# A perceiver layer on one core: another table of pieces for the last units of cross-attention, and weights converted by ScalarE

## The chip, the cores and the metric

The kernel runs on one core of a Trainium2 chip. The metric is the device time of that core in microseconds. Times shown are medians of several runs; durations of single instructions come from one profiled execution.

## The reference, cut to what matters

Four batches of 256 query tokens (width 256) pass through three blocks, each with a residual sum. The arrays are float32.

```
x = x + cross_attention(layernorm(x), ctx, ctx)       # 16 heads of 16, 4096 context rows
x = x + feature_attention(layernorm(x))               # 16 heads, causal
x = x + feed_forward(layernorm(x))                    # hidden 768, int32 weights times 1/127
```

In feature attention queries and keys of each head are divided by their norm over the head's 16 numbers, `x / max(norm(x), 1e-12)`, then projected, shifted, clipped and exponentiated. The feed-forward weights `w_gate`, `w_up`, `w_down` come as int32 and are made float32 and scaled before their matmuls.

## The kernel before, in words

The work is written out in order by hand: TensorE (PE), VectorE (DVE), ScalarE (ACT) and SyncE (SP) run their instructions in the order of the source.

**Cross-attention** goes over 16 units (batch b, group q of four heads), each of 16 steps of 256 context rows, so there are 256 steps n = 0 to 255 and one more for what is left. In a step TensorE makes the scores `pt` (L741) and, 18 steps ahead of them, the products `pm` (L704) from which VectorE takes maxima (L711). ScalarE turns the scores into `e` by an exponential (L746). TensorE multiplies the `e` of the step before by the values into `pav` (L761), and VectorE sums it into `av` (L771, at a unit's first step L769). Steps from 238 on have no `pm`, because the last unit's maxima are done by then. The keys and values of later units are made between these, up to step 231. From step 232 one entry of the table `others` runs in each step; the table belongs to feature attention of batches 0 to 2, which is begun here, and its layer norms were done before. A unit's result is divided (`pt_x` L787, L791, L793) two steps into the next unit.

The pieces of the table, for batch b with tiles 2b and 2b+1 of 128 tokens:

- `turn`: four transposes of the normed rows (L198), copied by VectorE (L199).
- `qk(i)`: the matmuls `pqk` (L207), the bias by VectorE (L211), and the squares on GpSimd (L213).
- `sq(i)`: sums of squares by head, VectorE (L216).
- `v`: the matmuls of the values (L225), biases by VectorE (L230).
- `normed_pair(b)`: `normed` for both tiles, 13 small VectorE instructions (L241, L123 to L129, L245) that turn the sums of squares into inverse norms by shifts and three iterations.
- `qk_normed(t)`: queries and keys of a tile times their inverse norms, VectorE (L249).
- `qk_turned(t)`: four transposes (L254), copied by VectorE (L255).
- `features(n)`: sixteen matmul instructions into four banks `pf` (L271), clipped by VectorE (L277), exponentials on ScalarE (L278), a factor on GpSimd (L279).

In PSUM, `bank` gives out eight banks of one pool in turn, so a tile waits until the one eight allocations before it has been read.

**Attention and feed-forward** follow in 16 steps `attend(n)` and one more. TensorE makes `pa` (L407, L412), VectorE masks it into `at` (L417), TensorE makes `po` (L426), ScalarE copies it to `avT` (L431), TensorE turns that (`pt_o`, L438) and VectorE divides (L440 to L442). Between the steps lie the lists `fills[n]`: in `fills[1]` to `fills[3]` the weights are converted by `weight(0)` to `weight(2)` (L390), in `fills[2]` and `fills[3]` the last projection of cross-attention is finished (`px` L811 with its copy L812, `py` L819, sum L822) and the layer norm of batch 3 is made (L139 to L147, which contain the same small iterations L123 to L129), in `fills[4]` the turn and queries and keys of batch 3 follow. All three weights arrive through the one buffer `w_i`; a load (L51) is issued on SP's queue, and the next one only when the conversion before it has read the buffer.

Of the kernel before, what the change touches and what calls it, by code (L numbers as in the profile page):

```python
# [14 lines left out]
AF = mybir.ActivationFunctionType  # L15
ALU = mybir.AluOpType
# [23 lines left out]
def perceiver_layer(  # L40
# [5 lines left out]
    nc = tc.nc  # L46
# [69 lines left out]
    def inverse_root(v):  # L116


        y = lnp.tile(list(v.shape), F32, tag=f"ir_y{v.shape[1]}", name="ir_y")
        t = lnp.tile(list(v.shape), F32, tag=f"ir_t{v.shape[1]}", name="ir_t")  # L120

        def first():
            nc.vector.tensor_scalar(y.bitcast(I32), v.bitcast(I32), 1, None, ALU.arith_shift_right)  # L123
            nc.vector.tensor_scalar(y.bitcast(I32), y.bitcast(I32), -1, 0x5F3759DF, ALU.mult, ALU.add)

        def better():
            nc.vector.tensor_tensor(t, y, y, ALU.mult)
            nc.vector.scalar_tensor_tensor(t, t, -0.5, v, ALU.mult, ALU.mult)
            nc.vector.scalar_tensor_tensor(y, t, 1.5, y, ALU.add, ALU.mult)  # L129

        return y, [first, better, better, better]
# [106 lines left out]
    def normed(tiles):  # L238

        some = nrm[:, tiles[0] : tiles[-1] + 1, :].rearrange("p t h -> p (t h)")  # L240
        nc.vector.tensor_scalar(some, some, 1e-24, None, ALU.max)  # L241
        y, pieces = inverse_root(some)
        for piece in pieces:
            piece()
        nc.vector.tensor_copy(some, y)  # L245
# [35 lines left out]
    def start_causal():  # L281


        zs = [causal_in(b) for b in range(B - 1)]
        n = 2 * (B - 1)
        mv = lnp.tile([P, n, 2], F32, tag="ln_mv6", name="ln_mv6", bufs=1)
        v = lnp.tile([P, n], F32, tag="ln_v6", name="ln_v6", bufs=1)
        rs, roots = inverse_root(v)
        s2 = lnp.tile([P, R], F32, tag="s2", name="s2", bufs=1)
        rs2, roots2 = inverse_root(s2)  # L290

        def constants():


            nc.gpsimd.memset(va, 1.0)
            nc.vector.tensor_scalar(top, rest[6], 20.0, None, ALU.add)
            nc.vector.tensor_scalar(low, rest[6], -20.0, None, ALU.add)
            nc.vector.tensor_scalar(shift, rest[6], -1.0, None, ALU.mult)
            nc.vector.tensor_scalar(fac, rest[7], 0.0, 1.0 / M, ALU.max, ALU.mult)
            nc.vector.tensor_scalar(s2, rest[10][:, : R * M : M], 0.0, 2.0, ALU.max, ALU.mult)  # L300

        def scaled():

            nc.vector.tensor_tensor(s2, s2, rs2, ALU.mult)
            om = rest[5].rearrange("p k (r m) -> p (k r) m", m=M)
            for i in range(4):
                to = om[:, R * i : R * i + R, :]
                nc.vector.tensor_tensor(to, to, s2.unsqueeze(2).to_broadcast([P, R, M]), ALU.mult)

        def stats(t):  # L310
            st = lnp.tile([P, 6], F32, tag="ln_st", name="ln_st")
            nc.vector.bn_stats(st, xr[:, t, :])
            nc.vector.bn_aggr(mv[:, t, :], st)
            nc.vector.tensor_scalar(v[:, t : t + 1], mv[:, t, 1:2], LN_EPS, None, ALU.add)

        def normal(t):
            nc.vector.tensor_scalar(
                zs[t // 2][5][:, t % 2, :], xr[:, t, :], mv[:, t, 0:1], rs[:, t : t + 1], ALU.subtract, ALU.mult
            )
            nc.gpsimd.tensor_tensor(xr[:, t, :], xr[:, t, :], rest[9], ALU.add)  # L320

        norms = (
            [lambda t=t: stats(t) for t in range(n)] + roots + [lambda t=t: normal(t) for t in range(n)]
            + [constants] + roots2 + [scaled]
        )

        (_, turn0, qk0, sq0, v0, _), (_, turn1, qk1, sq1, v1, _), (_, turn2, qk2, sq2, v2, _) = zs

        def normed_pair(b):
            return lambda: normed((2 * b, 2 * b + 1))  # L330

        def call(f, *args):
            return lambda: f(*args)

        others = [
            [turn0],
            [call(qk0, 0)],
            [call(qk0, 1), call(sq0, 0)],
            [v0, call(sq0, 1)],
            [turn1, normed_pair(0)],  # L340
            [call(qk1, 0), call(qk_normed, 0)],
            [call(qk1, 1), call(sq1, 0), call(qk_normed, 1)],
            [v1, call(sq1, 1)],
            [call(qk_turned, 0), normed_pair(1)],
            [call(qk_turned, 1), turn2, call(qk_normed, 2)],
            [call(features, 0), call(qk_normed, 3)],
            [call(features, 2)],
            [call(qk2, 0)],
            [call(qk2, 1), call(sq2, 0)],
            [v2, call(sq2, 1)],  # L350
            [call(qk_turned, 2), normed_pair(2)],
            [call(qk_turned, 3), call(qk_normed, 4)],
            [call(qk_turned, 4), call(qk_normed, 5)],
            [call(qk_turned, 5)],
            [call(features, 4)],
        ]
        return norms, [call(lambda pieces: [piece() for piece in pieces], pieces) for pieces in others]

    finish = cross_attention(
        tc, xr, load_x, load_rest, ctxT, wq_sb, bq_sb, wkP, bk_sb, wvP, eps, ident, layernorm, transposed,  # L360
        qT, kts, lnp, bank, rest, start_causal)
    wout_sb = rest[8]

# [19 lines left out]
    coming = []  # L383

    def weight_load(i):
        src = (w_gate, w_up, w_down)[i]
        coming.append(load(src, list(ws[i].shape), "w_i", mybir.dt.int32, nc.sync, late))

    def weight(i):
        nc.gpsimd.tensor_scalar(ws[i], coming[i], (1.0, 0.5, 1.0)[i] / 127.0, None, ALU.mult)  # L390
        if i + 1 < len(ws):
            weight_load(i + 1)

# [115 lines left out]
    with tc.manual_schedule(engines={ET.PE, ET.Activation, ET.DVE, ET.SP}):  # L509
# [4 lines left out]
        fills = {n: [] for n in range(NB + 1)}  # L514
        norm3, turn3, qk3, sq3, v3, _ = causal_in(3)
        fills[1] += [lambda: weight(0)]
        fills[2] += [turn15, lambda: weight(1)]
        fills[3] += [project15, norm3, lambda: weight(2)]
        fills[4] += [turn3, lambda: qk3(0)]
        fills[5] += [lambda: qk3(1), lambda: sq3(0), v3, lambda: sq3(1), lambda: normed((6, 7))]  # L520
# [4 lines left out]
        def call(b, part, *args):  # L525
            return lambda: ff[b][part](*args)
# [531 lines left out]
```

## Time and profile before

| what | value |
|---|---|
| median of 3 runs | 1243.35 us (1241.18 to 1244.96) |
| profiled execution, its own time | 1243.55 us |
| its span, first to last instruction | 1241.8 us |
| mean granted TensorE clock | 0.989 |
| TensorE matmuls, busy | 1205.1 us (97%) |
| VectorE, busy | 932.3 us (75%) |
| ScalarE, busy | 669.6 us (54%) |
| GpSimd, busy | 71.4 us (6%) |
| first piece of `others`, step 232 | about 987 us |
| last unit, steps 240 to 255 | 1029.87 us to about 1084 us |
| conversions of the weights on GpSimd | 3 of 4.09 us, from 1096.0, 1104.3 and 1112.6 us |

Times inside the profile count from the first instruction of the span. A row of a timeline has start, length, engine, line, operation, output and inputs, and in brackets how long the engine was idle before it and what ended that. The granted clock is the share of full speed that TensorE had.

### The profile page before, as it was taken

How to read it: one execution, taken by the hardware profiler on the slowest of the kernel's cores; microseconds unless marked ns; L12 is line 12 of the kernel's file. 1: busy time of each engine (PE TensorE's matmuls, PEld its weight loads, DVE VectorE, ACT ScalarE, POOL GpSimd, SP SyncE). 2: the span in 40 equal slices, each digit the busy share in tenths (PEclk: the TensorE clock that was granted, in tenths of full speed). 3: DMA queues.
4: the chain of work that ended last, by engine and by line, in shares of the span. 5: the costliest groups of instructions: out<-in, count | busy, mean ns of one | idle time of the engine just before them, and what ended most of it. 6: DMA issues, size and time to landing. Idle time of an engine off the chain costs nothing.

```text
span 1241.8 us, 42115 instructions
## 1 busy us (share of the span) xinstructions
PE 1205.1 (97%) x17712; PEld 809.0 (65%) x17712; DVE 932.3 (75%) x1823; ACT 669.6 (54%) x1391; POOL 71.4 (6%) x118
## 2 busy tenths in 40 slices
PE   6999999999999999999999999999999999969998
PEld 3566667666766676667666766677667745536777
DVE  4787777777777777777777777777788866597763
ACT  2446666666665656566566666666566536731311
POOL 4010000000000000000000000000001012151100
PEclk8999999999999999999999999999999989989999
DMA  6351342233223322332233223322332000020000
GB/s 227 105 179 59 103 117 71 60 103 105 85 60 102 114 77 58 102 107 80 61 94 101 87 68 90 102 89 72 88 103 88 5 1 4 2 79 1 9 10 18
DMA packets 57756, 95.78 MB, mean 77 GB/s; under 512 B 29024, under 2 KB 31712, under 8 KB 57568
## 3 DMA queue, kind: packets, MB, share of 16 engines
q1 hardware_dynamic: 56384, 92.17, 24.5%
q8 instruction: 140, 2.29, 0.8%
q10 hardware_dynamic: 672, 0.92, 0.2%
q14 instruction: 48, 0.39, 0.1%
q0 software_dynamic: 512, 0.00, 0.0%
HBM read 74.17 MB, written 1.05 MB: 61 GB/s over the span
## 4 chain that ended last, share of the span: by engine, by line
PE 91%; DVE 5%; ACT 1%; issue 1%; DMA 1%; SPq 0%; ACTq 0%; POOL 0%; DVEq 0%
PE pt L741 21%; PE pm L704 18%; PE pav L761 18%; PE pv L668 10%; PE pk L638 10%; PE pd L500 2%; PE pg L488 1%; PE pu L488 1%; PE pqk L207 1%; PE pq L844 1%; PE po L426 1%; DVE at L417 1%; PE pa L407 1%; PE py L462 1%; DVE kt L277 1%
## 5 line engine op out<-in xcount | busy, mean ns | idle before, releaser
L711 DVE TENSOR_REDUCE mx<-pm 128x1 f32<-128x512 f32 x1024 | 636.0, 684 | 146.6 <-PE pm L704 146.6
L746 ACT ACTIVATE e<-pt 128x512 f32<-128x512 f32 x1024 | 528.9, 603 | 390.1 <-PE pm L704 363.8
L704 PE MATMUL pm<-kt,qT 32*128 32x512 f32 x2048 | 500.3, 618 | 4.7 <-ACT ku L646 2.4
L741 PE MATMUL pt<-qa,kt 32*128 32x256 f32 x4096 | 501.1, 388 | 1.2 <-DVE qa L727 1.0
L741 PEld LDWEIGHTS pt<-qa,kt 32*128 32x128 f32 x4096 | 316.4, 184 | 118.4 <-ACT v L675 43.2
L761 PE MATMUL pav<-e,v 128*32 128x256 f32 x4096 | 270.3, 380 | 0.0
L704 PEld LDWEIGHTS pm<-kt,qT 32*128 32x128 f32 x2048 | 172.1, 184 | 22.5 <-issue 4.9
L761 PEld LDWEIGHTS pav<-e,v 128*32 128x32 f32 x4096 | 128.9, 110 | 74.6 <-ACT e L746 5.1
L771 DVE TENSOR_TENSOR av<-pav,av 128x256 f32<-128x256 f32 x240 | 101.7, 424 | 64.8 <-PE pav L761 64.5
L638 PE MATMUL pk<-ctx,wk_sb 128*32 128x256 f32 x2048 | 138.6, 392 | 0.0
L668 PE MATMUL pv<-wv_sb,ctx 128*32 128x128 f32 x4096 | 137.5, 276 | 0.0
L668 PEld LDWEIGHTS pv<-wv_sb,ctx 128*32 128x32 f32 x4096 | 104.3, 109 | 43.9 <-DVE mx L711 43.1
L638 PEld LDWEIGHTS pk<-ctx,wk_sb 128*32 128x32 f32 x2048 | 55.3, 111 | 69.3 <-DVE mx L711 41.9
L646 ACT ACTIVATE ku<-pk,bk_sb 128x256 f32<-128x256 f32 x128 | 63.1, 495 | 15.2 <-PE pk L638 6.5
L798 POOL TENSOR_TENSOR on<-on,bv_sb 128x64 f32<-128x64 f32 x32 | 9.2, 308 | 816.5 <-DVE on L793 816.5
L675 ACT COPY v<-pv 128x256 f32<-128x256 f32 x128 | 51.8, 405 | 7.5 <-PE pv L668 7.5
L278 ACT ACTIVATE kt<-kt,shift 128x512 f32<-128x512 f32 x32 | 22.8, 724 | 30.1 <-DVE kt L277 30.1
L417 DVE TENSOR_TENSOR at<-pa,mask 128x384 f32<-128x384 f32 x64 | 31.1, 549 | 7.0 <-PE pa L412 7.0
L277 DVE TENSOR_SCALAR kt<-pf,low,top 128x512 f32<-128x512 f32 x32 | 23.7, 802 | 3.2 <-PE pf L271 3.2
L488 PE MATMUL pg<-zT,wg 128*128 128x256 f32 x96 | 23.0, 382 | 0.7 <-ACT zT L480 0.7
L492 ACT ACTIVATE th<-pg 128x512 f32<-128x512 f32 x12 | 7.1, 594 | 29.9 <-PE pg L488 29.9
L488 PE MATMUL pu<-zT,wu 128*128 128x256 f32 x96 | 22.7, 379 | 0.0
(126 smaller groups left out, 584.7 us busy)
## 6 DMA issues: line engine op xcount, KB each, us to landing
ctx<-in_ctxT_dram SPq DMA_DIRECT2D x128, 512.0 KB
kt<-ku SPq DMA_DIRECT2D x500, 32.0 KB
xo<-on SPq DMA_DIRECT2D x128, 8.0 KB
xr<-in_x_dram SPq DMA_DIRECT2D x4, 256.0 KB
out_dram<-o SPq DMA_DIRECT2D x8, 128.0 KB
wqkv_sb<-in_wqkv_dram SPq DMA_DIRECT2D x1, 768.0 KB
w_i<-in_w_gate_dram SPq DMA_DIRECT2D x1, 768.0 KB
w_i<-in_w_up_dram SPq DMA_DIRECT2D x1, 768.0 KB
```

The costliest lines, as they stand in the source:

```text
L417: nc.vector.tensor_tensor(at, pa, mask, ALU.mult)
L488: nc.tensor.matmul(ps[:, i, :], lhsT=w[:, k, ns], rhs=zT[:, k, :], start=k == 0, stop=k == KC - 1)
L638: nc.tensor.matmul(pk[32 * j : 32 * j + 32, :], lhsT=wk_sb[:, k, m * P + 32 * j : m * P + 32 * j + 32], rhs=x[:, k, cs], start=k == 0, sto ...
L646: nc.scalar.activation(ku[:, cs], made.pop(), AF.Identity, bias=bk_sb[:, m : m + 1])
L668: nc.tensor.matmul(pv[32 * j : 32 * j + 32, i, :], lhsT=x[:, k, t0 + 32 * j : t0 + 32 * j + 32], rhs=wv_sb[:, k, m * P : (m + 1) * P], sta ...
L675: nc.scalar.copy(to.rearrange("p t (h d) -> p t h d", d=HD + 1)[:, :, :, :HD], made.pop().rearrange("p t (h d) -> p t h d", d=HD),)
L704: nc.tensor.matmul(pm, lhsT=qT[rows, q, t0 : t0 + P], rhs=kt[rows, c * CH : (c + 1) * CH], start=True, stop=True,)
L711: nc.vector.tensor_reduce(mx[:, i, j, c : c + 1], pm, AX.X, ALU.max)
L741: nc.tensor.matmul(pt[:, i, :], lhsT=kt[rows, ks], rhs=qa[rows, :], start=True, stop=True)
L746: nc.scalar.activation(e, pt, AF.Exp, scale=0.25)
L761: nc.tensor.matmul(pav[32 * h : 32 * h + 32, :], lhsT=v[:, t % KT, c0 : c0 + 32], rhs=es[n, h][:, i, :], start=i == 0, stop=i == 1,)
L771: nc.vector.tensor_tensor(avs[u], pav, avs[u], ALU.add)
```

## The change

The table of pieces is another: `normed_pair` and `qk_normed` of the first three batches all stand in the last unit (entries 8 and later, steps 240 and later), with their turns and features moved to fit; entry 16 is empty. And `weight(i)` is computed by ScalarE as a scaled copy instead of by GpSimd.

```
@@ the table others, entries 4 and later
-            [turn1, normed_pair(0)],
-            [call(qk1, 0), call(qk_normed, 0)],
-            [call(qk1, 1), call(sq1, 0), call(qk_normed, 1)],
+            [turn1],
+            [call(qk1, 0)],
+            [call(qk1, 1), call(sq1, 0)],
             [v1, call(sq1, 1)],
-            [call(qk_turned, 0), normed_pair(1)],
-            [call(qk_turned, 1), turn2, call(qk_normed, 2)],
-            [call(features, 0), call(qk_normed, 3)],
-            [call(features, 2)],
-            [call(qk2, 0)],
+            [turn2, normed_pair(0)],
+            [call(qk2, 0), call(qk_normed, 0), call(qk_normed, 1)],
+            [call(qk_turned, 0), call(qk_turned, 1), normed_pair(1)],
+            [call(features, 0)],
+            [call(features, 2), call(qk_normed, 2), call(qk_normed, 3)],
             [call(qk2, 1), call(sq2, 0)],
             [v2, call(sq2, 1)],
-            [call(qk_turned, 2), normed_pair(2)],
-            [call(qk_turned, 3), call(qk_normed, 4)],
-            [call(qk_turned, 4), call(qk_normed, 5)],
-            [call(qk_turned, 5)],
+            [call(qk_turned, 2), call(qk_turned, 3), normed_pair(2)],
+            [],
+            [call(qk_normed, 4), call(qk_normed, 5)],
             [call(features, 4)],
+            [call(qk_turned, 4), call(qk_turned, 5)],
         ]
@@ weight(i)
-        nc.gpsimd.tensor_scalar(ws[i], coming[i], (1.0, 0.5, 1.0)[i] / 127.0, None, ALU.mult)
+        nc.scalar.activation(ws[i], coming[i], AF.Copy, scale=(1.0, 0.5, 1.0)[i] / 127.0)
         if i + 1 < len(ws):
             weight_load(i + 1)
```

## The prediction

> **What bounds the kernel now.** I read the busy shares first: TensorE's row has 97%, VectorE's 75%, ScalarE's 54%, and in the chain that ended last TensorE holds 91%. So only what stops or slows TensorE can move the end. Then I read the clock row of the 40 slices. It falls below 9 in two places, and both are where the diff works. Windows cut at the start of steps 237, 238, 239 and 240 of cross-attention, and one over attention's start, show them (columns: stretch, length, busy time of PE, PEld, DVE, ACT, POOL, granted clock, DMA):
>
> ```profile
> 1010.33:1021.51 11.18, 8.92 (x48) 3.48 (x44) 7.38 (x22) 2.17 (x4) 0.28 (x1) 0.69 0.01 1
> 1021.51:1025.87 4.36, 4.36 (x42) 2.02 (x38) 1.96 (x6) 2.07 (x4) 1.50 (x2) 1.00 0.00 0
> 1025.87:1029.87 4.00, 4.00 (x41) 2.58 (x40) 2.72 (x7) 2.06 (x4) 0.62 (x1) 1.00 0.00 0
> ...
> 1084.42:1124.83 40.41, 27.84 (x228) 17.85 (x228) 31.79 (x69) 10.64 (x18) 21.35 (x22) 0.83 0.19 61
> ```
>
> Step 237 takes 11.18 us. Step 233 holds the same TensorE work (scores, maxima, one `pqk`) and took 4.96 us in another such window. The timeline says why (start, length, instruction, idle time before it and its releaser):
>
> ```profile
> 1010.99 0.18 DVE L241 TENSOR_SCALAR nrm<-nrm 128x64 f32<-128x64 f32 x1
> ...
> 1014.00 0.20 DVE L245 COPY nrm<-ir_y 128x64 f32<-128x64 f32 x1
> 1014.11 0.42 DVE L771 TENSOR_TENSOR av<-pav,av 128x256 f32<-128x256 f32 x1
> ...
> 1014.58 1.21 PE L704 MATMUL pm<-kt,qT 32*128 32x512 f32 x1 [2.26 <-DVE av L771]
> ...
> 1016.58 3.78 PE L207 MATMUL pqk<-wqkv_sb,zT 128*128 128x512 f32 x4
> ```
>
> The 13 instructions of `normed` (L241 to L245) hold VectorE for 3.1 us; the sum behind them (L771) empties a PSUM bank that `pm` needs; TensorE stands 2.26 us, and then `pqk` runs 3.78 us where it takes 1.98 elsewhere. In attention:
>
> ```profile
> 1091.33 0.35 ACT L431 COPY avT<-po 128x256 f32<-128x256 f32 x1
> ...
> 1096.00 4.09 POOL L390 TENSOR_SCALAR wg<-w_i 128x1536 f32<-128x1536 int32 x1 [4.01 <-DMA w_i<-in_w_gate_dram]
> ...
> 1100.48 0.35 ACT L431 COPY avT<-po 128x256 f32<-128x256 f32 x1
> ...
> 1104.30 4.09 POOL L390 TENSOR_SCALAR wu<-w_i 128x1536 f32<-128x1536 int32 x1 [4.21 <-DMA w_i<-in_w_up_dram]
> ...
> 1104.43 3.98 DVE L124 TENSOR_SCALAR ir_y<-ir_y 128x2 int32<-128x2 int32 x1
> ...
> 1112.49 2.07 PE L271 MATMUL pf<-qT,om_sb 32*128 32x256 f32 x10 [7.01 <-DVE at L417]
> ```
>
> Two columns of VectorE work last 3.98 us, exactly until GpSimd's conversion of `wu` ends; TensorE stands 7.01 us behind it.
>
> **What the Trainium skill says.** (1) "SBUF — State Buffer", section "SBUF: two separate sides": VectorE (in its two-port modes) and GpSimd share a port pair under an exclusive lock that the first holds for its whole instruction; ScalarE has its own. The 3.98 us agree. (2) "TensorE: Matmul & The Clock Gate", "What's actually happening": the clock halves after an idle window of about 3.4 us and returns after a busy one, and windows run free. Narrow windows agree: the clock is 0.50 from 1013.97 to 1020.8, two windows of 3.41. But the window that dropped it was still about half busy; stops of 1.5 and 1.6 us (before 1091.73 and 1100.88) dropped nothing. (3) "ScalarE: Activation LUTs", "What ACT_TABLE_LOAD costs": 186 ns + 0.833 ns per element for immediate scale, so 1.47 us for 1536. The trace's 1024-element copy (L899) took 1.034 us, which fits.
>
> **The change, part one: the table.** No instruction is added or removed; the moved ones issue no DMA, and SP and POOL keep their order except for the squares of `qk2`'s first half, which come earlier.
> Step 237 loses the 3.1 us of VectorE: 11.18 becomes 4.96, −6.2 (2.3 + 1.5 of standing, the rest half clock). Steps 238 and 239 keep their TensorE work: 0.
> Steps 240 to 244, 19.36 us before, I replayed by hand, in times of before. Pieces: scores 1.07, `pav` 1.00, `pqk` 1.92, one `tr_qk` or turn 0.6, `pf` 1.0, `pt_x` 0.4; eight banks in turn, so a tile waits for the one eight allocations earlier. 240: turn 2.67, VectorE in `normed` to 1035.4. 241: `pqk`, 4.0. 242: two `tr_qk` and `pt_x`, 3.6, to 1040.1. VectorE then does two copies and the second `normed` until 1042.6 and the sum and division until 1043.4, and the third and fourth `pf` of step 243 need those banks: TensorE stands about 1.5 + 0.4 us, and 243 takes 5.2. 244 (features, two L249): 4.0. Sum 19.4: the stop is paid for by stops of the old order that are gone. 245 and 246 are unchanged.
> From 247 to the last `pav`: the third `normed` stops step 249's scores for 1.3 us, but features(4) comes a step earlier. From there ScalarE is the bound: six groups of exponentials at 2.06 and four L278 (2.65) make 15.0 us, started at 1066.5 instead of 1067.3, and with fewer gaps: −1.0.
> Sum of part one −7.2; half a clock drop behind 243's stop (one window of 3.4 us costs up to 1.7, covered in part by VectorE) +0.5: **−6.7**.
>
> **Part two: the weights.** Removed: 3 × 4.09 us on POOL and the lock: 3.8 on L124 and four later operations at 0.42 instead of 0.16, so 4.8 us of VectorE. Added: 3 × 1.47 on ScalarE, in order, each waiting for a DMA. `wg` lands at 1096.0, so the second `avT` (L431) behind it goes from 1093.45 to 1097.4, and `pt_o`, `pf` and VectorE's L277 behind that come 2.5 to 3 us late (TensorE stands 3.0; its clock probably drops). SP issues `w_up` at 1097.5; it lands 4.2 us later, hidden by L278, which ends at 1102.7. `wu` runs to 1104.2, so the third `avT` is at 1104.2, not 1100.48; `project15` and its sum (L822) at 1106.0 instead of 1102.5. The norm takes 4.75 us from there instead of 9.4: L417 starts at 1110.75 against 1111.89: −1.1. `wd` (issue 1104.3, landing 1108.5) frees the fourth `avT` at 1110.3, before VectorE wants it. With a halved clock from 1098 on the chain is 0.8 later. Both ends: −1.1 to +2.3 (clock low throughout). I take **−0.3**. Behind `w_down` SP has only outputs 50 us later; features(8)'s L279 on POOL come earlier, and nobody waits for them.
>
> Sum −7.0. The profiled execution took 1243.55 (span 1241.8 + 1.75 around it), 0.2 over the median: 1236.5 less that 0.2 is 1236.4.
>
> **The rivals.**
> A, as worked out: 1236.4, its own range 1233 to 1240. 66%.
> B, ScalarE's waits cost more than the lock: stops at `wg` and `wu` keep the clock low until 1118; `pf`, `px`, `po`, `pa` and `py` behind `wg` take 10 us instead of 5, L417 starts 2.3 late, so −6.7 + 2.3: 1239.0. For it: any 3 us stop fills most of a window. Against: VectorE bounds this stretch. 13%.
> C, the table does not do what it says: 237 stays long because its four maxima and bias additions (L711, L211), not `normed`, hold the bank. Then only −1.0 and −0.3 remain: 1242.1. Against: steps 233 to 235 have both and run at 4.9. 6%.
> D, slower: the stall only moves. If the second and third `normed` each stop TensorE for 2.3 us, in 243 and 249, instead of 1.5 and 1.3, the clock falls both times and each costs the 6.2 us seen in 237: −6.2 + 12.4 − 0.3 gives 1249.3. It decides from about 1.7 us idle within one window. Against: no maxima wait in these steps, and 240 to 242 held one `normed` before with 0.24 us of stop. 8%.
> E, the clock stays up and the gaps close: −6.2, −2.0 after step 247, −1.1, and the 1.9 us of standing in 243 gone: 1232.2. 7%.
>
> **How the numbers follow.** What a measurement here tells from no change is 0.3%, 3.7 us. Faster by that: most of A, half of B, E: 0.77. Within: the rest of A and B, and C: 0.15. Slower: D, 0.08. Range 1232 to 1242: from E to C, leaving out D.
>
> **What would show it.** Right: step 237 near 5 us at clock 1.00; 240 to 244 near 19.4, with one `pf` wait of 1.5 to 2 us on L771; L124 at 0.17 to 0.2 us everywhere; L390 on ACT at 1.47; a TensorE wait of about 3 us on `avT` near 1091; 1084.42 to 1124.83 (40.4 us) within a microsecond. Wrong: a clock of 0.5 in steps 243 to 250, or attention's start over 42 us. The whole forecast falls if 237 stays above 7 us.

## The result and the profile after

The changed kernel takes 1236.09 us (median of 5 runs, 1233.88 to 1238.65) against 1243.35 of the kernel before on the same chip (5 runs, 1241.18 to 1244.96): a ratio of 0.9942, 95% interval 0.9924 to 0.9960, so 7.2 us less. The profiled execution took 1238.65, the longest of the five, with a span of 1236.9 and a mean granted clock of 0.993.

First the windows of the changed kernel, cut at the same places as before: step 237; steps 240 to 244; steps 245 and 246; from step 247 to attention's start; and from there to the first `po` of the fifth step (columns: stretch, length, busy time of PE, PEld, DVE, ACT, POOL, granted clock, DMA share, GB/s). The last seven lines cut attention along a grid of 3.41 us, of which more at the end.

```profile
1012.85:1017.93 5.08, 5.08 (x48) 2.83 (x44) 4.24 (x8) 2.06 (x4) 0.06 (x1) 1.00 0.01 3
1026.29:1046.06 19.77, 18.71 (x214) 10.68 (x210) 16.75 (x46) 12.82 (x24) 3.83 (x7) 1.00 0.04 5
1046.06:1054.35 8.29, 8.29 (x80) 4.68 (x77) 5.71 (x12) 6.71 (x13) 4.07 (x5) 1.00 0.02 2
1054.35:1081.54 27.19, 25.98 (x341) 14.94 (x337) 14.22 (x35) 20.93 (x40) 2.33 (x5) 1.00 0.01 2
1081.54:1119.95 38.41, 25.45 (x229) 16.30 (x229) 27.33 (x69) 14.65 (x21) 9.39 (x19) 0.96 0.19 64
...
1090.09:1093.50 3.41, 1.95 (x23) 1.41 (x17) 2.14 (x5) 0.64 (x1) 0.00 (x0) 1.00 0.50 204
1093.50:1096.91 3.41, 2.26 (x28) 1.41 (x32) 1.39 (x4) 1.10 (x2) 0.00 (x0) 1.00 0.39 144
1096.91:1100.33 3.42, 1.92 (x28) 1.43 (x20) 3.42 (x7) 3.24 (x5) 1.70 (x4) 1.00 0.21 86
1100.33:1103.74 3.41, 2.09 (x24) 1.34 (x24) 2.42 (x8) 1.27 (x2) 0.21 (x1) 1.00 0.44 139
1103.74:1107.15 3.41, 1.51 (x17) 1.23 (x16) 2.89 (x17) 1.74 (x2) 0.00 (x0) 1.00 0.23 94
1107.15:1110.57 3.42, 2.67 (x22) 1.61 (x22) 3.35 (x10) 0.00 (x0) 1.51 (x2) 1.00 0.02 5
1110.57:1113.98 3.41, 0.31 (x1) 0.30 (x2) 3.04 (x5) 2.88 (x4) 1.49 (x4) 1.00 0.00 0
```

The reader sees step 237 at 5.08 us with TensorE busy all through it, where it was 11.18 at a clock of 0.69, and attention's start at 38.41 us and clock 0.96, where it was 40.41 and 0.83. The three stretches between them are not shorter. Cut in the same way in every kernel (from the first `pt` of a step, `pt_x` of the last unit and `po` of attention's fifth step), the table of stretches is, in us:

| kernel | 237 | 240 to 246 | 247 to attention | attention's start |
|---|---|---|---|---|
| before | 11.18 | 27.34 | 27.20 | 40.42 |
| changed | 5.08 | 28.06 | 27.19 | 38.41 |
| changed, second profile | 5.09 | 28.06 | 27.18 | 38.38 |
| table alone | 5.09 | 28.06 | 27.18 | 40.09 |
| weights alone | 11.50 | 27.35 | 27.20 | 40.41 |
| before, GpSimd in quarters | 9.85 | 27.35 | 27.20 | 36.87 |
| changed, weights one list later | 5.09 | 28.06 | 27.18 | 37.20 |
| new table, GpSimd in quarters | 5.09 | 28.06 | 27.18 | 36.20 |

All else is level, but for the first unit. In the changed kernel's profile the clock is 0.50 from 83.16 to 89.98, far from any edit, and step 237 starts at 1012.85 where it started at 1010.34. So the two spans, 4.9 apart, are 7.4 of gain less 2.5 lost at the start. The second profile of the same kernel has no such loss: step 237 starts at 1008.74, and its span is 1232.8, so nearly all of the 4.1 us between these two profiles lies at the start. The kernel before lost clock at its start too, from 24.10 to 30.93: its clock row has an 8 in the first slice, a third low place beside the two that the prediction counted.

The timeline of the changed kernel (start, length, engine, instruction, idle time before it and its releaser), first around steps 237, 242 and 243, then after step 247, then in attention:

```profile
1015.02 1.98 PE L207 MATMUL pqk<-wqkv_sb,zT 128*128 128x512 f32 x4
...
1032.73 2.13 DVE L249 TENSOR_TENSOR kt<-kt,nrm 128x512 f32<-128x512 f32 x2
1032.96 1.35 POOL L213 TENSOR_TENSOR sq<-kt 128x512 f32<-128x512 f32 x1 [10.05 <-DVE kt L211]
...
1038.80 0.69 PE L271 MATMUL pf<-qT,om_sb 32*128 32x256 f32 x2 [0.31 <-ACT e L746]
1039.43 0.42 DVE L771 TENSOR_TENSOR av<-pav,av 128x256 f32<-128x256 f32 x1
1039.90 1.12 PE L271 MATMUL pf<-qT,om_sb 32*128 32x256 f32 x10 [0.41 <-DVE av L771]
...
1064.21 2.06 ACT L746 ACTIVATE e<-pt 128x512 f32<-128x512 f32 x4 [0.41 <-PE pt L741]
...
1071.06 2.06 ACT L746 ACTIVATE e<-pt 128x512 f32<-128x512 f32 x4 [0.37 <-PE pt L741]
1073.53 4.14 ACT L746 ACTIVATE e<-pt 128x512 f32<-128x512 f32 x8 [0.41 <-PE pt L741]
...
1092.86 1.48 ACT L390 ACTIVATE wg<-w_i 128x1536 f32<-128x1536 int32 x1 [4.06 <-DMA w_i<-in_w_gate_dram]
1094.24 0.35 ACT L431 COPY avT<-po 128x256 f32<-128x256 f32 x1
...
1094.65 0.44 PE L438 MATMUL pt_o<-ident,avT 128*128 128x128 f32 x2 [2.61 <-ACT avT L431]
...
1099.88 1.47 ACT L390 ACTIVATE wu<-w_i 128x1536 f32<-128x1536 int32 x1
...
1101.65 0.44 PE L438 MATMUL pt_o<-ident,avT 128*128 128x128 f32 x2 [2.82 <-ACT avT L431]
1102.99 0.42 DVE L822 TENSOR_TENSOR xr<-py,xr 128x256 f32<-128x256 f32 x1
1104.94 0.17 DVE L124 TENSOR_SCALAR ir_y<-ir_y 128x2 int32<-128x2 int32 x1
...
1107.56 1.95 DVE L417 TENSOR_TENSOR at<-pa,mask 128x384 f32<-128x384 f32 x4
...
1113.67 3.51 PE L207 MATMUL pqk<-wqkv_sb,zT 128*128 128x512 f32 x4 [3.79 <-DVE zT L199]
```

`pqk` of step 237 takes 1.98 us, not 3.78, and nothing waits before it. In attention one wait of 7.0 us has become two of 2.6 and 2.8. PE's list of waits (engine, operation, releaser: us in total, times, longest), of which one line stands below, shows the exchange: `pf` behind `at`, 7.0 before, is gone, as is `pm` behind `av`, 2.3 before, and `pt_o` behind ScalarE's `avT` has grown from 3.7 us to 9.5.

```profile
PE pt_o L438 <- ACT avT L431: 9.5, 5, 2.8
```

### The profile page after: what moved, and what is told of

Same layout as the page of the kernel before. It is cut to its first block, busy times and chain, and to the rows that moved or that the text cites. A ratio compares the mean times of both kernels' runs of the same rounds, so it can differ in the third digit from the quotient of the medians.

```text
span 1236.9 us, 42097 instructions
## 1 busy us (share of the span) xinstructions
PE 1200.7 (97%) x17712; PEld 808.3 (65%) x17712; DVE 928.3 (75%) x1823; ACT 673.2 (54%) x1394; POOL 60.2 (5%) x115
## 4 chain that ended last, share of the span: by engine, by line
PE 92%; DVE 4%; DMA 1%; ACT 1%; issue 1%; SPq 0%; ACTq 0%; POOL 0%; DVEq 0%
PE pt L741 22%; PE pm L704 18%; PE pav L761 18%; PE pv L668 11%; PE pk L638 10%; PE pd L500 2%; PE pg L488 1%; PE pu L488 1%; PE pq L844 1%; PE pqk L207 1%; PE po L426 1%; PE pa L407 1%; PE py L819 1%; PE py L462 1%; PE pf L271 0%
## 5 line engine op out<-in xcount | busy, mean ns | idle before, releaser
L711 DVE TENSOR_REDUCE mx<-pm 128x1 f32<-128x512 f32 x1024 | 636.1, 684 | 149.2 <-PE pm L704 149.1
L417 DVE TENSOR_TENSOR at<-pa,mask 128x384 f32<-128x384 f32 x64 | 31.1, 549 | 7.0 <-PE pa L412 7.0
```

Source lines behind the costliest of these rows:

```text
L417: nc.vector.tensor_tensor(at, pa, mask, ALU.mult)
L711: nc.vector.tensor_reduce(mx[:, i, j, c : c + 1], pm, AX.X, ALU.max)
```

## The experiments

The medians of the kernel before, run beside these kernels, were 1242.2 to 1243.8 us. Each ratio is against the runs of the kernel before on the same chip. It is not the ratio of the medians: the two differ by up to 0.0022 in what follows.

**The table alone** (the weights stay on GpSimd):

```
-        nc.scalar.activation(ws[i], coming[i], AF.Copy, scale=(1.0, 0.5, 1.0)[i] / 127.0)
+        nc.gpsimd.tensor_scalar(ws[i], coming[i], (1.0, 0.5, 1.0)[i] / 127.0, None, ALU.mult)
```

> The new table alone, the weights still on GpSimd. Theory: the two parts add, and the table gives what the traces show for steps 237 to 255: 237 takes 5.1 us instead of 11.2, steps 240 to 246 cost 0.7 us more, the rest is level, so about 5.4 us faster than before (1238), with L124 still at 4 us in attention. The prediction's own sum for this part was 6.7 us. Rival: most of the gain is ScalarE's conversion, and the table gives 3 us or less.

Measured: 1236.56 us, ratio 0.9965 (0.9952 to 0.9979). Step 237 is 5.09, attention's start 40.09. The timeline of this kernel shows the same lock with another victim:

```profile
1096.10 4.02 DVE L123 TENSOR_SCALAR ir_y<-ln_v 128x2 int32<-128x2 int32 x1
1100.15 0.43 DVE L124 TENSOR_SCALAR ir_y<-ir_y 128x2 int32<-128x2 int32 x1
...
1104.40 2.07 PE L271 MATMUL pf<-qT,om_sb 32*128 32x256 f32 x10 [7.04 <-DVE at L417]
```

Here `wu` runs on GpSimd from 1096.00 to 1100.09, and L123, one instruction earlier than L124, lasts 4.02 us; L124 itself is 0.43. TensorE's wait of 7.04 us is unchanged. So the lock falls on whichever small instruction comes next, and the table alone brings the gain of step 237 and next to nothing in attention. L124's 0.43, like the four operations at 0.42 of the kernel before, lies beside GpSimd's short instructions L279, which come right after the conversion (from 1108.37 in the kernel before): not all of the 4.8 us of VectorE that the prediction put down to the conversions was held by a conversion itself.

**The weights alone** (old table):

```
-        nc.gpsimd.tensor_scalar(ws[i], coming[i], (1.0, 0.5, 1.0)[i] / 127.0, None, ALU.mult)
+        nc.scalar.activation(ws[i], coming[i], AF.Copy, scale=(1.0, 0.5, 1.0)[i] / 127.0)
```

> ScalarE converts the weights, the old table kept. Theory from the traces: attention's start takes 38.4 us instead of 40.4, so 2.0 us faster (1241.4), step 237 still 11.2 us. The prediction said 0.3 us faster, with a loss of up to 2.3 us if TensorE's clock falls behind the wait for wg. A measured gain over 1 us with the clock at 1.00 behind wg settles it for the first, a loss with a clock of 0.5 there for the second.

Measured: 1241.29 us, ratio 0.9997 (0.9983 to 1.0011). The median is 1.7 us under that of the kernel before beside it (1243.0), the ratio level, and no change lies in the interval: a gain of a microsecond or two is neither shown nor excluded. Attention's start is 40.41, as before. The windows of this kernel say where the gain went:

```profile
1096.23:1099.64 3.41, 1.32 (x18) 0.92 (x18) 0.66 (x3) 1.74 (x2) 0.00 (x0) 1.00 0.27 40
...
1099.64:1103.05 3.41, 3.41 (x28) 1.87 (x26) 3.14 (x5) 2.23 (x4) 0.95 (x2) 0.50 0.47 191
...
1116.71:1123.53 6.82, 6.10 (x12) 3.27 (x13) 1.32 (x3) 1.59 (x4) 1.99 (x3) 0.50 0.00 0
```

TensorE's stop before `pt_o` was 3.54 us here, 2.1 us of it lay within one window (1.32 of 3.41 busy), and the clock was halved in the next one and again for two windows later, 10.24 us in all. In the changed kernel it was halved for 3.41. The stop was longer because `wg` landed later: ScalarE waited 4.99 us for it, 4.06 in the changed kernel, and SP's eight transfers `xo` (L802), behind which the load of `w_gate` is issued, took 5.95 us instead of 5.28. Whether the old table has a part in that, one profile can't tell.

**GpSimd in quarters** (the kernel before, each conversion in four instructions):

```
-        nc.gpsimd.tensor_scalar(ws[i], coming[i], (1.0, 0.5, 1.0)[i] / 127.0, None, ALU.mult)
+        to, frm = (w.rearrange("p n m -> p (n m)") for w in (ws[i], coming[i]))
+        for j in range(4):
+            part = slice(384 * j, 384 * j + 384)
+            nc.gpsimd.tensor_scalar(to[:, part], frm[:, part], (1.0, 0.5, 1.0)[i] / 127.0, None, ALU.mult)
```

> The kernel before, with each conversion on GpSimd cut into four instructions of 384 columns. Theory of the lock held for one instruction: L124 or another small VectorE instruction waits at most about 1.0 us at a time, the norm of batch 3 shortens by about 2 to 3 us, and the kernel is about 2 us faster than before although GpSimd does the same work. Rival (the 4 us of L124 come from something that lasts as long as the whole conversion, whatever its pieces): one instruction still takes about 4 us and the time is level.

Measured: 1239.56 us, ratio 0.9981 (0.9970 to 0.9993); attention's start is 36.87 instead of 40.42. (Step 237 is 9.85 in its profile with the stop unchanged: the halved clock behind it lasted one window of 3.41 us there, two in the kernel before.) The tile `w_i` of this kernel lists the conversion of `wu` (shortest, median and longest ns, first and last start):

```profile
L393 POOL TENSOR_SCALAR wu<-w_i x4: 1163/1190/1317, 1106.0 to 1109.5; 128x384 f32<-128x384 int32 x4
```

and line L124 of the same kernel, cut to attention, the instruction that had lasted 3.98 us:

```profile
L124 DVE TENSOR_SCALAR ir_y<-ir_y x2: 169/169/169, 1105.9 to 1124.8; 128x2 int32<-128x2 int32 x2
```

L124 ran just as the first piece began. The ones behind it ran beside the pieces, as VectorE's timeline shows:

```profile
1106.53 0.16 DVE L128 SCALAR_TENSOR_TENSOR ir_t<-ir_t,ln_v 128x2 f32<-128x2 f32 x1
...
1107.12 0.51 DVE L128 SCALAR_TENSOR_TENSOR ir_t<-ir_t,ln_v 128x2 f32<-128x2 f32 x1
1107.66 0.16 DVE L129 SCALAR_TENSOR_TENSOR ir_y<-ir_t,ir_y 128x2 f32<-128x2 f32 x1
...
1108.25 0.52 DVE L129 SCALAR_TENSOR_TENSOR ir_y<-ir_t,ir_y 128x2 f32<-128x2 f32 x1
```

Four pieces take 4.8 us, more than the one instruction of 4.09, yet the longest of these small instructions in this stretch is 0.52 us. So the price of the lock does not follow GpSimd's total work, and the rival is out. Nor does it follow the length of a piece: the two held longest start with the second and the third piece, and those between run in 0.16 us while a piece of 1.16 is under way. That the first holds the ports for its whole instruction, as the prediction had it, fits the uncut conversion and not the pieces; how the ports are granted within a piece is open. The cut shortens TensorE's stop before `pf` from 7.0 to 3.2 us without putting a DMA wait on ScalarE's queue.

**A shorter `normed`** (the kernel before, 7 of the 13 instructions):

```
-        for piece in pieces:
+        for piece in pieces[:2]:
             piece()
```

> The kernel before with one iteration instead of three in normed, so 7 of its 13 instructions stay (the inverse norms are rougher). Theory: normed's hold of VectorE falls from 3.1 to 1.6 us, TensorE's stop in step 237 falls below 1 us, the clock does not fall, the step takes about 5.5 us instead of 11.2 and the kernel is 5 to 6 us faster, by 1.6 us of VectorE work. Rival C of the prediction (maxima and bias additions hold the bank, not normed): step 237 stays above 9 us and the gain is 1.6 us at most.

Measured: 1234.71 us, ratio 0.9955 (0.9939 to 0.9971). Step 237 falls to 6.65 without any move in the table. Its timeline:

```profile
1010.29 0.20 DVE L245 COPY nrm<-ir_y 128x64 f32<-128x64 f32 x1
1010.39 0.42 DVE L771 TENSOR_TENSOR av<-pav,av 128x256 f32<-128x256 f32 x1
...
1010.87 0.69 PE L704 MATMUL pm<-kt,qT 32*128 32x512 f32 x1 [0.70 <-DVE av L771]
```

The stop before `pm` is 0.70 us where it was 2.26, and the clock stays at 1.00. The length of this one chain on VectorE set the stop, and the stop set the clock: the four maxima and biases of the step were there all the time. That is against C. The step is 1.2 us longer than the 5.5 expected. The kernel's gain is not step 237's alone, since each of these chains is shorter: steps 240 to 246 take 26.31 us instead of 27.34.

**A longer `normed`** (the changed kernel, the inverse root made twice in step 242):

```
-        y, pieces = inverse_root(some)
-        for piece in pieces:
-            piece()
+        for _ in range(2 if tiles[0] == 2 else 1):
+            y, pieces = inverse_root(some)
+            for piece in pieces:
+                piece()
```

> The changed kernel with the second normed (step 242) running its inverse root twice, the first result overwritten: 11 more small instructions, 2.7 us more of VectorE at that place. Rival D of the prediction (a stall that moves into the last unit costs what it cost in step 237, once it is long enough): TensorE stands over 3 us in step 243, the clock falls there for one or two windows of 3.41 us, and steps 240 to 244 grow from 19.8 to 24 us or more. Theory behind the forecast (the last unit has room): they grow by about 2.7 us or less and the clock stays at 1.00.

Measured, one execution: 1239.32 us, span 1237.6. Steps 240 to 246 take 33.78 us instead of 28.06. Eleven instructions more of 0.23 us are 2.5 us of VectorE; they can make at most that much of these 5.7, and the rest goes with the clock, as the windows of this kernel show:

```profile
1035.61:1039.02 3.41, 2.85 (x26) 1.40 (x22) 3.17 (x12) 0.31 (x1) 0.57 (x2) 1.00 0.02 5
1039.02:1049.26 10.24, 10.24 (x61) 5.97 (x57) 6.64 (x11) 9.20 (x16) 4.73 (x8) 0.50 0.07 6
```

So a longer chain in the last unit can cost what D said, some 2.5 us of VectorE away from the changed kernel. But the records don't show D's stop: in the window ahead of the fall TensorE is down as busy for 2.85 of 3.41 us, and the longest recorded wait is 0.54.

**The weights one list later** (the changed kernel, with `weight(0)` to `weight(2)` in `fills[2]` to `fills[4]`), so that `w_gate` has landed when ScalarE comes to it:

```
-        fills[1] += [lambda: weight(0)]
-        fills[2] += [turn15, lambda: weight(1)]
-        fills[3] += [project15, norm3, lambda: weight(2)]
-        fills[4] += [turn3, lambda: qk3(0)]
+        fills[2] += [turn15, lambda: weight(0)]
+        fills[3] += [project15, norm3, lambda: weight(1)]
+        fills[4] += [lambda: weight(2), turn3, lambda: qk3(0)]
```

> The changed kernel with weight(0), (1), (2) in fills 2, 3, 4 instead of 1, 2, 3, so that no copy avT stands behind the landing of w_gate. Theory (ScalarE's wait for wg, 2.6 to 3.5 us of TensorE, is on the path and its clock loss with it): the stretch from attention's start to the fifth po takes 35 to 36 us instead of 38.4, and the kernel is about 2.5 us faster than the changed one, ratio to before 0.992. Rival (VectorE bounds this stretch and covers the wait): 38 us, ratio as the changed kernel's 0.9942.

Measured: 1235.18 us, ratio 0.9942 (0.9929 to 0.9956), level with the changed kernel; attention's start in the profile is 37.20, between the two expectations. The timeline of this kernel:

```profile
1097.61 1.47 ACT L390 ACTIVATE wg<-w_i 128x1536 f32<-128x1536 int32 x1
...
1099.38 0.44 PE L438 MATMUL pt_o<-ident,avT 128*128 128x128 f32 x2 [2.96 <-ACT avT L431]
...
1103.31 1.48 ACT L390 ACTIVATE wu<-w_i 128x1536 f32<-128x1536 int32 x1 [3.98 <-DMA w_i<-in_w_up_dram]
```

`wg` no longer waits for its DMA, yet TensorE still stands 2.96 us behind ScalarE, at the third `avT`, and `wu` now waits 3.98. With one buffer `w_i` each load starts only after the conversion before it, so the wait moves to the next weight. Two other ways out were not tried: a buffer for each weight, and issuing the load of `w_gate` ahead of the eight transfers `xo`. In the changed kernel these hold SP's queue from 1083.12 to 1088.40, the load follows at 1088.52, and `wg` starts at 1092.86.

**Features two steps earlier** (the changed kernel, `features(4)` in the empty entry 16):

```
-            [],
-            [call(qk_normed, 4), call(qk_normed, 5)],
             [call(features, 4)],
+            [call(qk_normed, 4), call(qk_normed, 5)],
+            [],
```

> The changed kernel with features(4) in the empty entry 16 (step 248) instead of entry 18. It asks why the 1.0 us that the prediction saw from step 247 on did not come. If ScalarE bounds the end of the unit, work given to it two steps earlier, where it stood idle about 1 us a step, ends it sooner: 247 to attention 26 to 26.5 us instead of 27.2. If the turn of eight banks between scores and exponentials sets the pace, it stays within 0.3 us of 27.2 or grows, because four pf banks come on top of the third normed.

Measured: 1237.93 us, ratio 0.9957 (0.9942 to 0.9972). From step 247 to attention it takes 27.53, not less than 27.19. Giving ScalarE its exponentials earlier gains nothing there, which speaks against its load as the pace of this stretch. It isn't proof, since the four banks of `pf` now come on top of the third `normed` and may cost what the earlier start gains. In this profile the clock fell in step 243, for one window, though steps 240 to 247 hold the same work as in the changed kernel:

```profile
1034.02:1037.43 3.41, 2.69 (x28) 1.39 (x28) 2.84 (x11) 2.12 (x5) 0.57 (x2) 1.00 0.02 5
...
1037.43:1040.84 3.41, 3.41 (x36) 2.36 (x28) 2.40 (x4) 3.32 (x6) 1.91 (x4) 0.50 0.13 12
```

Steps 240 to 246 took 28.27 us with it, 28.06 without: 0.2 us. A clock of 0.5 in these steps was one of the prediction's signs of being wrong; it comes with this table in some executions, and is cheap.

**The new table with GpSimd in quarters** (the two edits that had each gained, together), against the changed kernel:

```
-        nc.scalar.activation(ws[i], coming[i], AF.Copy, scale=(1.0, 0.5, 1.0)[i] / 127.0)
+        to, frm = (w.rearrange("p n m -> p (n m)") for w in (ws[i], coming[i]))
+        for j in range(4):
+            part = slice(384 * j, 384 * j + 384)
+            nc.gpsimd.tensor_scalar(to[:, part], frm[:, part], (1.0, 0.5, 1.0)[i] / 127.0, None, ALU.mult)
```

> The new table with the weights on GpSimd in four instructions each. Theory (the parts add; the lock costs by the length of one instruction; GpSimd waits for the DMAs where nobody stands behind it): attention's start takes about 37 us as in the kernel before with quarters, against 38.4 to 40.4 with ScalarE, so about 9 us faster than before and 1.5 to 3 us faster than the changed kernel: ratio 0.992 to 0.993. Rival (ScalarE's conversion is the better half of the change): not faster than the changed kernel, 0.994 or more.

Measured: 1232.43 us, ratio 0.9917 (0.9905 to 0.9930). It was run once more beside the changed kernel on one chip:

> The table with the weights on GpSimd in quarters again. If it is better than the changed kernel and not lucky, it is 1.5 to 4 us below it on the same chip, with attention's start at 36 to 37 us. If its first time was the clock's phase, the two are within 1 us.

> The changed kernel again, beside the table with quarters on one chip. The clock windows run free, so attention's start should land anywhere from 38.4 us (clock kept behind wg) to 40.4 us (clock lost), with every step from 237 to the last of the unit as in its first trace to 0.1 us unless a window closes in it; ratio to before 0.993 to 0.996.

There it took 1233.16 us (1232.52 to 1235.22), ratio 0.9916 (0.9896 to 0.9935), against 1236.17 (1234.50 to 1239.16), ratio 0.9939 (0.9920 to 0.9959), of the changed kernel. It beats the kernel before by some 10 us and the changed one by 3.0 in these medians, though the two intervals overlap. Attention's start in the second profile is 36.63. The timeline of the first, in attention:

```profile
1089.06 4.58 POOL L393 TENSOR_SCALAR wg<-w_i 128x384 f32<-128x384 int32 x4 [4.22 <-DMA w_i<-in_w_gate_dram]
...
1093.73 0.44 PE L441 MATMUL pt_o<-ident,avT 128*128 128x128 f32 x2 [1.59 <-ACT avT L434]
...
1098.96 0.51 DVE L127 TENSOR_TENSOR ir_t<-ir_y 128x2 f32<-128x2 f32 x1
...
1101.34 2.07 PE L271 MATMUL pf<-qT,om_sb 32*128 32x256 f32 x10 [3.00 <-DVE at L420]
```

GpSimd waits for the DMA, and behind that wait stands nobody that TensorE needs. TensorE's stop of 7.0 us before `pf` is 3.0, and `pt_o` waits 1.6 as in the kernel before.

## Why the prediction was right

It said 1236.4 and A; measured were 1236.1 and A. Its terms by the profiles (us):

| step of the prediction | said | measured |
|---|---|---|
| step 237 | −6.2 | −6.1 |
| steps 238 and 239 | 0 | 0.0 |
| steps 240 to 244 | 0.0 | +0.4 |
| steps 245 and 246 | 0 | +0.3 |
| 247 to the last `pav` | −1.0 | 0.0 |
| clock behind step 243 | +0.5 | 0 here, +0.2 with features earlier |
| the weights | −0.3 | −2.0 here, 0.0 alone |

The sum is better than its parts. The table gave −5.4 where −6.7 was said, the weights −2.0 where −0.3 was said, and the two misses cancel to 0.4 us: in that measure the number was luck. A's own range also holds B's 1239.0, so it is the profiles that tell the two apart.

**Step 237** went as worked out, and two independent edits (move the chain away, or shorten it) show its mechanism. Its size was right because another step with the same TensorE work gave the length. The split that the prediction gave of it is not borne out: of its 2.3 + 1.5 us of standing the matmul records show the 2.26 alone (8.92 busy of 11.18); 1.5 is what the weight load of `pqk` waited for a maximum (L711). The matmuls took 8.92 us where the changed kernel's take 5.08, so by the records some 3.8 us, not 2.4, go with the halved clock.

**Steps 240 to 244** were a replay by hand: 2.67, 4.0, 3.6, 5.2, 4.0, against 2.67, 3.99, 3.98, 5.03, 4.10. The term that was off is step 242. The replay gave the two L249 their usual 0.68 us each; they took 2.13 together, the second 1.53, because GpSimd's squares (L213) ran in the middle of them. The kernel before had shown it: there an L249 beside L213 took 1.22 (at 1025.81). The Trainium skill, "SBUF — State Buffer", section "SBUF: two separate sides", counts VectorE operations with two SBUF inputs among those that the lock blocks; L249 has two, and the trace agrees. The prediction had used the lock for L124 alone. In step 243 the expected stop of 1.5 + 0.4 us is recorded as 0.31 + 0.41 although the step lasted nearly what was said: records of matmuls end where they are modelled to end, and so a step's length is the better witness than its stops.

**247 to the last `pav`** is where a step failed: "ScalarE is the bound". The group of exponentials that should have come 0.8 us earlier came 0.2 earlier (9.86 us after step 247 began, at 1064.21, against 10.04), ScalarE then stood 0.37, 0.41 and 0.18 us for `pt`, and moving its work two steps ahead gave nothing. What sets the pace there instead, no run isolated. The stop of the third `normed` in step 249 was forecast at 1.3 us and is recorded as 0.69; the same caution holds for it.

**The weights** had every landmark close: TensorE stood 2.61 us (3.0 said), `wu` had no wait, from L822 to L417 it took 4.57 us (4.75), and L417 came 1.45 us earlier counted from attention's start (1.1). The term that was mis-sized is the clock: "its clock probably drops". In the two profiles of the changed kernel it did not drop behind `wg`, and at the end it was low for 3.41 us instead of 13.65. Counted on TensorE the gain lies there: it stood as long as before in this stretch (12.6 us without a matmul before, 13.0 after), and its matmuls took 2.4 us less.

That the clock held was luck of the moment. With the longer `normed`, whose lists in attention are the same, the stop behind `wg` was 2.82 us and the next window ran at half clock:

```profile
1093.63:1097.04 3.41, 1.47 (x19) 0.95 (x19) 1.11 (x4) 1.74 (x2) 0.00 (x0) 1.00 0.19 45
1097.04:1100.46 3.42, 3.42 (x30) 2.08 (x28) 3.30 (x5) 2.45 (x4) 1.16 (x3) 0.50 0.46 185
```

Yet attention's start took 38.37 us there, against 38.41 and 38.38 in the two profiles with the clock held: TensorE stood 1.26 us before the third `pt_o` instead of 2.82. With features earlier the clock fell behind `wg` too, after a stop of 2.64 us where the second profile of the changed kernel held it after 2.63; it was low for 13.65 us in two pieces, and the stretch took 39.51. So B's low clock came in two of four profiles with these lists, for less long than B said, and none was over the 40.4 of the kernel before. The weights alone had it for 10.24 us, with a stop of 3.54, and gained nothing. The two ends of the term were +2.3 and −1.1, and the stretch was to stay within a microsecond of 40.4; the profiles lie from 0 to −2.0, and how much of that spread is the clock and how much the later landing of `wg` with the weights alone is not settled. By their ratios the weights alone and the table alone add up to −4.7, the change to −7.2; by their medians they add up to −8.1. The intervals of the ratios (±1.7 to ±2.2) leave open whether the parts simply add.

**Where the stops fell** can be read off the seven grid lines. "TensorE: Matmul & The Clock Gate", "What's actually happening", has windows of about 3.4 us that run free of the kernel, and every stretch of half clock in the profiles of all kernels here, the first 20 us and the last stretch, cut by the end, left out, was a whole number of 3.41 us long (3.41, 6.83, 10.24 or 13.65). Counted back from the fall at 1113.98, the stop of 2.61 us (1092.04 to 1094.65) lies across the edge at 1093.50 and that of 2.82 across 1100.33. Each window keeps at least 1.5 us of work, and none drops the clock; the first with less, 0.31, does. In the kernel with the weights alone the stop is longer and leaves one window only 1.32, which drops it. The page speaks of an idle window; here windows with 1.09 to 1.76 us recorded as busy dropped it too, and even those with 2.41 (before 83.16), 2.69 and 2.85, while one with 1.51 did not. So the recorded busy time does not give the rule, and how the chip counts is open.

## What to carry to other kernels

A long chain on VectorE is best put where no PSUM bank waits behind it: the same 3.1 us cost 6 us in step 237, and steps 240 to 246, which hold two of these chains since the change and held one before, grew by 0.7. Don't put an instruction that waits for a DMA on an in-order engine whose next instruction feeds TensorE; an engine with no such follower, in short pieces if it shares a lock, gave medians 3 us lower here. Price a stop of 1.5 to 3 us twice, with the clock held and with it lost, because the place of the stop in a free-running window decides between them; and ask whether TensorE would have stood soon after anyway, since behind `wg` one lost window then cost nothing that shows.

## What the runs showed that was not expected

- One GpSimd instruction of 4.09 us held a small VectorE instruction for 3.93 to 4.02 us; four of 1.16 held none over 0.52, less than half of a piece.
- A window recorded as busy for 2.69 of 3.41 us went before a halved clock in one kernel; in the changed kernel one as full (the grid's 1107.15 to 1110.57, 2.67) did not.
- Executions of one kernel differ by several us: those of the changed kernel by 4.7 and 4.8, those of the kernel before by up to 9.7. In the profiles most of that lies in the first unit, where the clock is lost in some and not in others: step 16 started between 141.2 and 146.8 us over kernels that are alike up to there, and the three that started it at 146.0 or later are those with a clock of 0.50 from about 83 to 90 us.
